# Non-local attention on one core: query tiles in pairs on halves of TensorE, and a constant in place of the row maximum

## The chip, the cores and the metric

The kernel runs on one core of one Trainium2 chip. The core has TensorE (PE, matrix multiply, which writes to the accumulator memory PSUM), VectorE (DVE, elementwise work and reductions), ScalarE (ACT, functions such as exp), GpSimd (POOL) and the queues that start DMA transfers. The metric is the device time of one execution in microseconds (us), lower being better. The median of three runs of the kernel before is 6832.08 us (6814.51 to 6840.58).

## The reference: what is computed

Two layers of a "non-local block" on `x` of shape (4, 128, 96, 96): four images of 128 channels and 96 x 96 = 9216 pixels, all in f32. One layer, with its own weights:

```
g_x     = maxpool2(g_w @ x + g_b)          # 64 channels x 2304 pooled pixels: the values
theta_x = theta_w @ x + theta_b            # 64 channels x 9216 pixels: the queries
phi_x   = maxpool2(phi_w @ x + phi_b)      # 64 channels x 2304 pooled pixels: the keys
f       = theta_x^T phi_x                  # 9216 x 2304 scores
attn    = softmax(f) over the 2304 keys
y       = attn g_x^T                       # 9216 x 64
out     = (W_w @ y + W_b) * inv + (bn_beta - bn_mean * inv) + x     # inv = bn_gamma / sqrt(bn_var + 1e-5)
```

The second layer takes the first one's output. The scores and the product with the values are nearly all the work: 2 x 64 x 9216 x 2304 multiplications for each layer and image. A softmax is unchanged when one number is subtracted from all scores of a row, or when one vector is subtracted from all keys.

## The kernel before, in words

An image stays on chip through both layers; the four images follow each other, and the next one's load is started a whole image early. `block` does one layer of one image, so there are eight blocks.

A block begins with `keys_and_values`: 24 matmuls (`gphi_ps`, L128) give g and phi for 384 pixels each, ACT adds the bias (`full`, L132), DVE takes the 2 x 2 maximum in two steps (`half`, `gphi`). `spread` (L143) copies phi to the other half of the partitions (`phi1`) and transposes g into `gT`, 18 tiles of 128 keys, each with 64 columns of g and 64 columns of ones.

Then come 18 query tiles of 512 pixels. A tile goes through two stages:

- `stage1`: theta (L172); the scores with queries on partitions, 24 matmuls of 64 rows x 384 columns (`max_ps`, L179), in pairs of which one takes partitions 0 to 63 (`phi`) and the other 64 to 127 (`gphi`); DVE reduces each to a row maximum (`mx`, L188); four transposes turn the negated maximum into a 65th row of theta (`m_ps`, L198; L199).
- `stage2`: for each of 18 key tiles the scores again, now with keys on partitions (`sc`, L246, 65 rows, so that the maximum is subtracted), exp on ACT (L250), and the product with `gT` into the accumulator `av` (L260). Its columns of ones give the softmax denominators on partitions 64 to 127.

`finish` takes four reciprocals (L217), multiplies (`y`, L220), projects with W (`W_ps`, L224) and adds shift and residual (L225). The order is written out by hand: in `stage2` the step for key tile k issues the scores of tile k+1, then the steps of `finish` for the tile before and of `stage1` for the tile after that are due at k (the dictionaries `steps`), then the product for tile k. A scheduler keeps this order on each engine except at the borders between blocks, where it moves work that is ready ahead. Every f32 matmul appears in the trace as two records of TensorE, each with its own weight load.

Of the kernel before, what the change touches and what calls it, by code (L numbers as in the profile page):

```python
# [8 lines left out]

F32 = mybir.dt.float32  # L10
AF = mybir.ActivationFunctionType
ALU = mybir.AluOpType
AX = mybir.AxisListType
PSUM = bass.MemoryType.PSUM

P = 128
B, C, CI, H, W = 4, 128, 64, 96, 96
HW = H * W
NK = (H // 2) * (W // 2)
QT = 512  # L20
NQ = HW // QT
KT = 128
NKT = NK // KT
GT = 6
CC = 4 * W
MC = 384
NMC = NK // MC
BN_EPS = 1e-5
PARAMS = ["g_w", "g_b", "theta_w", "theta_b", "phi_w", "phi_b", "W_w", "W_b",
          "bn_gamma", "bn_beta", "bn_mean", "bn_var"]  # L30


@with_exitstack
def nonlocal_blocks(ctx: ExitStack, tc: tile.TileContext, x: bass.AP, layers, out: bass.AP):
    """Two non-local blocks over 4 images; an image stays on chip through both.

    A query tile of 512 pixels goes through two stages:
      1. theta, the scores with queries on partitions, and their row maximum m;
      2. the scores with keys on partitions, -m added by a 65th contraction row, exp,
         and the product with g^T, whose 64 columns of ones give the denominators  # L40
         on 64 partitions.
    Stage 1 of a tile is interleaved with stage 2 of the tile before it.
    """
    nc = tc.nc

    const = ctx.enter_context(tc.tile_pool(name="const", bufs=1))
    prep = ctx.enter_context(tc.tile_pool(name="prep", bufs=2))
    xp = ctx.enter_context(tc.tile_pool(name="xp", bufs=2))
    yp = ctx.enter_context(tc.tile_pool(name="yp", bufs=1))
    kvp = ctx.enter_context(tc.tile_pool(name="kvp", bufs=2))  # L50
    work = ctx.enter_context(tc.tile_pool(name="work", bufs=3))
    ps_max = ctx.enter_context(tc.tile_pool(name="ps_max", bufs=3, space=PSUM))
    ps_sc = ctx.enter_context(tc.tile_pool(name="ps_sc", bufs=2, space=PSUM))
    ps_av = ctx.enter_context(tc.tile_pool(name="ps_av", bufs=2, space=PSUM))
    ps_misc = ctx.enter_context(tc.tile_pool(name="ps_misc", bufs=1, space=PSUM))

    ident = const.tile([P, P], F32, name="ident")
    make_identity(nc, ident)
    eps = const.tile([P, 1], F32, name="eps")
    nc.vector.memset(eps, BN_EPS)  # L60

    def load_x(b):
        xt = xp.tile([C, HW], F32, tag="x", name=f"x_{b}")
        src = x[b].rearrange("c h w -> c (h w)")
# [51 lines left out]
        return w  # L116

    def keys_and_values(xt, w, name):
        """g^T beside columns of ones, and phi on both halves of the partitions."""
        gphi = kvp.tile([P, NK], F32, tag="gphi", name=f"gphi_{name}")  # L120
        phi1 = kvp.tile([CI + 1, NK], F32, tag="phi1", name=f"phi1_{name}")
        gT = kvp.tile([P, NKT, 2 * CI], F32, tag="gT", name=f"gT_{name}")
        nc.gpsimd.memset(phi1[CI:, :], 1.0)
        nc.gpsimd.memset(gT[:, :, CI:], 1.0)

        def pooled(r):
            ps = ps_sc.tile([P, QT], F32, tag="sc", name=f"gphi_ps_{name}_{r}")
            nc.tensor.matmul(  # L128
                ps[:, :CC], lhsT=w["gphi"], rhs=xt[:, ts(r, CC)], start=True, stop=True
            )  # L130
            full = work.tile([P, CC], F32, tag="full", name=f"full_{name}_{r}")
            nc.scalar.activation(full, ps[:, :CC], AF.Identity, bias=w["gphi_b"])  # L132
            half = work.tile([P, CC // 2], F32, tag="half", name=f"half_{name}_{r}")
            fv = full.rearrange("p (n d) -> p n d", d=2)
            nc.vector.tensor_max(half, fv[:, :, 0], fv[:, :, 1])
            hv = half.rearrange("p (h d w) -> p h d w", d=2, w=W // 2)
            nc.vector.tensor_max(
                gphi[:, ts(r, CC // 4)].rearrange("p (h w) -> p h w", w=W // 2),
                hv[:, :, 0],
                hv[:, :, 1],  # L140
            )

        def spread(i):  # L143
            keys = ts(i, GT * KT)
            nc.scalar.copy(phi1[:CI, keys], gphi[CI:, keys])
            ps = ps_max.tile([P, QT], F32, tag="mx", name=f"gT_ps_{name}_{i}")
            for j in range(GT):
                nc.tensor.transpose(  # L148
                    ps[:, ts(j, CI)], gphi[:CI, ts(i * GT + j, KT)], ident[:CI, :CI]
                )  # L150
            nc.vector.tensor_copy(
                gT[:, ts(i, GT), :CI],
                ps[:, : GT * CI].rearrange("p (t c) -> p t c", c=CI),
            )

        per = GT * KT * 4 // CC
        for r in range(HW // CC):
            pooled(r)
            if r % per == 0 and r:
                spread(r // per - 1)  # L160
        spread(NKT // GT - 1)
        return gphi, phi1, gT

    def stage1(xt, w, phis, name):
        """The query tile [theta; -m], and the steps that fill it."""
        th = work.tile([P, QT], F32, tag="theta", name=f"theta_{name}")
        mx = work.tile([P, QT // P, NMC], F32, tag="mxs", name=f"mx_{name}")
        nm = work.tile([P, QT // P], F32, tag="nm", name=f"nm_{name}")

        def theta():  # L170
            ps = ps_misc.tile([P, QT], F32, tag="misc", name=f"theta_ps_{name}")
            nc.tensor.matmul(ps, lhsT=w["theta"], rhs=xt, start=True, stop=True)  # L172
            nc.scalar.activation(th, ps, AF.Identity, bias=w["theta_b"])  # L173

        def pair(a, c):
            pss = []
            for h in range(2):
                ps = ps_max.tile([P, QT], F32, tag="mx", name=f"max_ps_{name}_{a}_{c + h}")
                nc.tensor.matmul(  # L179
                    ps[:, :MC],  # L180
                    lhsT=th[ts(h, CI), ts(a, P)],
                    rhs=phis[h][ts(h, CI), ts(c + h, MC)],
                    start=True,
                    stop=True,
                )
                pss.append(ps)
            for h in range(2):
                nc.vector.tensor_reduce(  # L188
                    mx[:, a, c + h : c + h + 1], pss[h][:, :MC], AX.X, ALU.max
                )  # L190

        def negmax():
            nc.vector.tensor_reduce(nm, mx, AX.X, ALU.max, negate=True)  # L193

        def row():
            ps = ps_misc.tile([P, QT], F32, tag="misc", name=f"m_ps_{name}")
            for a in range(QT // P):
                nc.tensor.transpose(ps[:1, ts(a, P)], nm[:, a : a + 1], ident)  # L198
            nc.scalar.copy(th[CI : CI + 1, :], ps[:1, :])  # L199

        steps = {0: theta}
        n = 2
        for a in range(QT // P):
            for c in range(0, NMC, 2):
                steps[n] = lambda a=a, c=c: pair(a, c)
                n += 1
        steps[n] = negmax
        steps[n + 2] = row
        return th, steps

    def finish(av, xt, w, dst, store, name):
        """The steps from the summed products to the block's output."""
        rc = work.tile([CI, QT], F32, tag="rc", name=f"rc_{name}")
        y = work.tile([CI, QT], F32, tag="y", name=f"y_{name}")

        def recip(i):
            nc.vector.reciprocal(rc[:, ts(i, P)], av[CI:, ts(i, P)])  # L217

        def norm():
            nc.vector.tensor_mul(y, av[:CI, :], rc)  # L220

        def project():
            ps = ps_misc.tile([P, QT], F32, tag="misc", name=f"W_ps_{name}")
            nc.tensor.matmul(ps, lhsT=w["W"], rhs=y, start=True, stop=True)  # L224
            nc.vector.scalar_tensor_tensor(  # L225
                dst, ps, w["shift"], xt, op0=ALU.add, op1=ALU.add
            )
            if store is not None:
                nc.sync.dma_start(out=store, in_=dst)

        steps = {i: (lambda i=i: recip(i)) for i in range(QT // P)}
        steps[QT // P] = norm
        steps[QT // P + 2] = project
        return steps
# [53 lines left out]
    xt = load_x(0)  # L288
    ws = [load_layer(l, p) for l, p in enumerate(layers)]
    for b in range(B):  # L290
        nxt = load_x(b + 1) if b + 1 < B else None
# [3 lines left out]
        xt = nxt  # L295


# [1 line left out]
_INS = ["x"] + [f"L{l}_conv_{p}" for l in range(2) for p in PARAMS]  # L299
_OUTS = [((B, C, H, W), "float32")]  # L300
# [25 lines left out]
```

## Time and profile before

| what | value |
|---|---|
| time, median of 3 runs | 6832.08 us (6814.51, 6832.08, 6840.58) |
| profiled execution, span from first to last instruction | 6810.1 us |
| TensorE busy | 6758.3 us, 99% |
| VectorE busy | 2595.4 us, 38% |
| ScalarE busy | 1862.6 us, 27% |
| DMA | 41.21 MB, mean 6 GB/s |
| mean granted clock of TensorE | 0.999 of full speed |

The profiled execution's page gives its span and no other time; by the three runs what lies around the span is between 4.4 and 30.5 us, and 22.0 us to the median. Records of matmuls overlap each other at their ends, so the length of a step on TensorE is read from the starts of successive records or from the chain of waits (which follows the work back from the last instruction and gives each piece only the time until the next begins), not from the mean duration.

### The profile page before, as it was taken

How to read it: one execution, taken by the hardware profiler on the slowest of the kernel's cores; microseconds unless marked ns; L12 is line 12 of the kernel's file. 1: busy time of each engine (PE TensorE's matmuls, PEld its weight loads, DVE VectorE, ACT ScalarE, POOL GpSimd, SP SyncE). 2: the span in 40 equal slices, each digit the busy share in tenths (PEclk: the TensorE clock that was granted, in tenths of full speed). 3: DMA queues.
4: the chain of work that ended last, by engine and by line, in shares of the span. 5: the costliest groups of instructions: out<-in, count | busy, mean ns of one | idle time of the engine just before them, and what ended most of it. 6: DMA issues, size and time to landing. Idle time of an engine off the chain costs nothing.

```text
span 6810.1 us, 48920 instructions
## 1 busy us (share of the span) xinstructions
PE 6758.3 (99%) x18966; PEld 2603.7 (38%) x18966; DVE 2595.4 (38%) x4889; ACT 1862.6 (27%) x3100; POOL 25.2 (0%) x22
## 2 busy tenths in 40 slices
PE   8999999999999999999999999999999999999999
PEld 3333333333333333333333333333333333333333
DVE  3333343333433334333343333433334333343333
ACT  2222232222322223222232222322223222222222
POOL 0000000000000000000000000000000000000000
PEclk9999999999999999999999999999999999999999
DMA  1000000000000000000000000000000000000000
GB/s 58 0 0 0 0 30 7 7 7 5 3 1 0 0 0 31 5 7 7 7 2 0 0 0 0 4 7 5 7 7 2 0 0 0 0 4 7 7 5 8
DMA packets 17065, 41.21 MB, mean 6 GB/s; under 512 B 4032, under 2 KB 4544, under 8 KB 16832
## 3 DMA queue, kind: packets, MB, share of 16 engines
q1 hardware_dynamic: 13824, 37.75, 1.5%
q8 instruction: 148, 2.42, 0.1%
q10 hardware_dynamic: 3008, 0.34, 0.0%
q14 instruction: 85, 0.70, 0.0%
HBM read 19.21 MB, written 18.87 MB: 6 GB/s over the span
## 4 chain that ended last, share of the span: by engine, by line
PE 99%; DVE 1%; DMA 0%; ACT 0%; issue 0%; ACTq 0%
PE av L260 37%; PE sc L246 33%; PE max_ps L179 22%; PE theta_ps L172 2%; PE gphi_ps L128 2%; PE W_ps L224 2%; PE m_ps L198 1%; DVE rc L217 0%; PE gT_ps L148 0%; DMA W_nat<-in_L_conv_W_w_dram 0%; DVE mx L188 0%; ACT full L132 0%; DMA theta_b<-in_L_conv_theta_b_dram 0%; DMA gphi_nat<-in_L_conv_phi_w_dram 0%; ACT theta L199 0%
## 5 line engine op out<-in xcount | busy, mean ns | idle before, releaser
L188 DVE TENSOR_REDUCE mx<-max_ps 128x1 f32<-128x384 f32 x3456 | 1763.8, 552 | 2804.5 <-PE max_ps L179 2800.0
L250 ACT ACTIVATE exp<-sc 128x512 f32<-128x512 f32 x2592 | 1547.7, 597 | 4696.7 <-PE sc L246 4696.7
L260 PE MATMUL av<-exp,gT 128*128 128x512 f32 x5184 | 2796.9, 625 | 0.0
L246 PE MATMUL sc<-theta,phi 65*128 65x512 f32 x5184 | 2628.6, 592 | 5.9 <-ACT theta L199 5.9
L179 PE MATMUL max_ps<-gphi,theta 64*128 64x384 f32 x3456 | 1570.6, 535 | 0.0
L179 PE MATMUL max_ps<-phi,theta 64*128 64x384 f32 x3456 | 1556.3, 531 | 4.0 <-DVE mx L188 3.1
L246 PEld LDWEIGHTS sc<-theta,phi 65*128 65x128 f32 x5184 | 986.3, 190 | 1247.0 <-issue 1213.4
L260 PEld LDWEIGHTS av<-exp,gT 128*128 128x128 f32 x5184 | 835.0, 188 | 1295.3 <-ACT exp L250 866.8
L179 PEld LDWEIGHTS max_ps<-phi,theta 64*128 64x128 f32 x3456 | 518.9, 185 | 1230.1 <-DVE mx L188 958.0
L217 DVE RECIPROCAL rc<-av 64x128 f32<-64x128 f32 x576 | 488.7, 908 | 1003.0 <-PE av L260 1003.0
L179 PEld LDWEIGHTS max_ps<-gphi,theta 64*128 64x128 f32 x3456 | 508.6, 184 | 18.1 <-DVE mx L188 16.7
L224 PE MATMUL W_ps<-y,WT 64*128 64x512 f32 x288 | 162.6, 644 | 4.2 <-DVE y L220 4.2
L132 ACT ACTIVATE full<-gphi_ps,gphi_b 128x384 f32<-128x384 f32 x192 | 110.7, 581 | 73.2 <-PE gphi_ps L128 50.3
L225 DVE SCALAR_TENSOR_TENSOR out<-W_ps,shift,y 128x512 f32<-128x512 f32 x72 | 54.0, 751 | 164.3 <-PE W_ps L224 164.3
L225 DVE SCALAR_TENSOR_TENSOR y<-W_ps,shift,x 128x512 f32<-128x512 f32 x72 | 54.1, 751 | 162.5 <-PE W_ps L224 162.5
L199 ACT COPY theta<-m_ps 1x512 f32<-1x512 f32 x144 | 82.5, 573 | 106.3 <-PE m_ps L198 103.0
L173 ACT ACTIVATE theta<-theta_ps,theta_b 128x512 f32<-128x512 f32 x144 | 99.0, 688 | 30.5 <-PE theta_ps L172 30.5
L220 DVE TENSOR_TENSOR y<-av,rc 64x512 f32<-64x512 f32 x144 | 98.2, 682 | 4.9
L198 PE MATMUL m_ps<-ident,nm 128*1 128x128 f32 x576 | 86.4, 271 | 6.9 <-DVE nm L193 6.9
L128 PE MATMUL gphi_ps<-x,gphiT 128*128 128x384 f32 x192 | 82.7, 542 | 7.6 <-ACT full L132 4.7
L224 PEld LDWEIGHTS W_ps<-y,WT 64*128 64x128 f32 x288 | 42.6, 185 | 111.9 <-issue 103.1
L198 PEld LDWEIGHTS m_ps<-ident,nm 128*1 128x1 f32 x576 | 47.0, 83 | 99.5 <-issue 80.0
(40 smaller groups left out, 598.0 us busy)
## 6 DMA issues: line engine op xcount, KB each, us to landing
x<-in_x_dram SPq DMA_DIRECT2D x24, 768.0 KB, 7.2
out_dram<-out SPq DMA_DIRECT2D x72, 256.0 KB, 2.0
theta_nat<-in_L_conv_theta_w_dram ACTq DMA_DIRECT2D x4, 32.0 KB, 5.3
theta_b<-in_L_conv_theta_b_dram ACTq DMA_DIRECT2D x4, 0.2 KB, 5.8
gphi_nat<-in_L_conv_g_w_dram ACTq DMA_DIRECT2D x2, 32.0 KB, 5.3
gphi_nat<-in_L_conv_phi_w_dram ACTq DMA_DIRECT2D x2, 32.0 KB, 4.2
W_nat<-in_L_conv_W_w_dram ACTq DMA_DIRECT2D x2, 32.0 KB, 7.4
gphi_b<-in_L_conv_g_b_dram ACTq DMA_DIRECT2D x2, 0.2 KB, 5.1
```

Of the source, the lines that this page charges most:

```text
L128: nc.tensor.matmul(ps[:, :CC], lhsT=w["gphi"], rhs=xt[:, ts(r, CC)], start=True, stop=True)
L132: nc.scalar.activation(full, ps[:, :CC], AF.Identity, bias=w["gphi_b"])
L172: nc.tensor.matmul(ps, lhsT=w["theta"], rhs=xt, start=True, stop=True)
L179: nc.tensor.matmul(ps[:, :MC], lhsT=th[ts(h, CI), ts(a, P)], rhs=phis[h][ts(h, CI), ts(c + h, MC)], start=True, stop=True,)
L188: nc.vector.tensor_reduce(mx[:, a, c + h : c + h + 1], pss[h][:, :MC], AX.X, ALU.max)
L198: nc.tensor.transpose(ps[:1, ts(a, P)], nm[:, a : a + 1], ident)
L217: nc.vector.reciprocal(rc[:, ts(i, P)], av[CI:, ts(i, P)])
L224: nc.tensor.matmul(ps, lhsT=w["W"], rhs=y, start=True, stop=True)
L225: nc.vector.scalar_tensor_tensor(dst, ps, w["shift"], xt, op0=ALU.add, op1=ALU.add)
L246: nc.tensor.matmul(ps, lhsT=phi1[:, ts(k, KT)], rhs=th[: CI + 1, :], start=True, stop=True)
L250: nc.scalar.activation(e, ps, AF.Exp)
L260: nc.tensor.matmul(av, lhsT=gT[:, k, :], rhs=es.pop(k), start=(k == 0), stop=(k == NKT - 1))
```

## The change

The kernel has a new main path, `shifted_blocks`. The old path is kept as `general_blocks`, word for word but for comments, and stands behind a branch.

- Two query tiles form a pair of 1024 queries. Theta of the first is written to partitions 0 to 63, of the second to 64 to 127 (`theta`). The scores of one key tile (`Pair.scores`) are two matmuls of 64 rows: phi on partitions 0 to 63 with the first tile, phi on 64 to 127 with the second; they fill a PSUM tile of 128 x 1024, and one exp covers both. The products (`Pair.values`) are two matmuls with 64 columns of `gT`: the first tile's go to partitions 0 to 63 of `av`, the second's to 64 to 127.
- The row maximum is not computed. Exp subtracts the constant 35, and phi is centred: the mean of its first 768 keys is subtracted from all. `stage1`'s 24 matmuls and reductions, the maximum's transposes and the 65th row are gone.
- The columns of ones are gone too: DVE sums the exp tiles (`sum`), one add of 128 x 1024 for each key tile but the first, and two matmuls with a matrix of ones (`denominators`) add them over the partitions. Reciprocals and `y` now cover 128 partitions, that is, a pair.
- DVE keeps the largest and smallest reciprocal (`rmax`, `rmin`). At the end they are compared with 1e20 and 1e-30, a flag is written, every engine loads it, and if it is above zero `general_blocks` runs and writes the output anew.
- Pooling is one DVE reduction out of PSUM; g's bias is added after pooling, phi's is left out. The first layer's output is written over `x` in place.
- The order by hand: batches of two key tiles. A step issues the scores of a batch, a W projection if due, then the products of the batch before, then theta or denominators if due.

```diff
+PT = 2 * QT
+NP = HW // PT
+KB = 2
+NB = NKT // KB
+SHIFT = 35.0
+SUM_MIN, SUM_MAX = 1e-20, 1e30
...
+    ps_sc = ctx.enter_context(tc.tile_pool(name="ps_sc", bufs=2, space=PSUM))
+    ps_av = ctx.enter_context(tc.tile_pool(name="ps_av", bufs=2, space=PSUM))
+    ps_misc = ctx.enter_context(tc.tile_pool(name="ps_misc", bufs=2, space=PSUM))
...
+        def pooled(r):
+            ps = ps_sc.tile([P, PT], F32, tag="sc", name=f"gphi_ps_{name}_{r}")
+            nc.tensor.matmul(
+                ps[:, :CC], lhsT=w["gphi"], rhs=xt[:, ts(r, CC)], start=True, stop=True
+            )
+            nc.vector.tensor_reduce(
...
+            if i == 0:
+                nc.vector.tensor_reduce(centre[CI:, :], gphi[CI:, keys], AX.X, ALU.add)
...
+            nc.scalar.activation(
+                phi[CI:, keys], gphi[CI:, keys], AF.Identity, bias=centre[CI:, :]
+            )
+            nc.scalar.copy(phi[:CI, keys], phi[CI:, keys])
...
+    def theta(xt, w, p, name):
+        ps = ps_misc.tile([P, QT], F32, tag="misc", name=f"theta_ps_{name}_{p}")
+        for h in range(2):
+            nc.tensor.matmul(
+                ps[ts(h, CI), :], lhsT=w["theta"], rhs=xt[:, ts(2 * p + h, QT)],
+                start=True, stop=True,
+            )
+        th = work.tile([P, QT], F32, tag="theta", name=f"theta_{name}_{p}")
+        nc.scalar.activation(th, ps, AF.Identity, bias=w["theta_b"])
...
+        def scores(self, k):
+            ps = ps_sc.tile([P, PT], F32, tag="sc", name=f"sc_{self.name}_{k}")
+            for h in range(2):
+                nc.tensor.matmul(
+                    ps[:, ts(h, QT)], lhsT=self.phi[ts(h, CI), ts(k, KT)],
+                    rhs=self.th[ts(h, CI), :], start=True, stop=True,
+                )
+            e = work.tile([P, PT], F32, tag="exp", name=f"exp_{self.name}_{k}", bufs=6)
+            nc.scalar.activation(e, ps, AF.Exp, bias=nshift)
+            self.es[k] = e
+            if k == 1:
+                self.sum = work.tile([P, PT], F32, tag="sum", name=f"sum_{self.name}")
+                nc.vector.tensor_add(self.sum, self.es[0], e)
+            elif k > 1:
+                nc.vector.tensor_add(self.sum, self.sum, e)
+
+        def values(self, k):
...
+            for h in range(2):
+                nc.tensor.matmul(
+                    self.av[ts(h, CI), :], lhsT=self.gT[:, k, :], rhs=e[:, ts(h, QT)],
+                    start=(k == 0), stop=(k == NKT - 1),
+                )
+
+        def denominators(self):
...
+            for i in range(QT // P):
+                nc.vector.reciprocal(rc[:, ts(i, P)], ps[:, ts(i, P)])
+            self.y = work.tile([P, QT], F32, tag="y", name=f"y_{self.name}")
+            nc.vector.tensor_mul(self.y, self.av, rc)
+            nc.vector.tensor_tensor(rmax, rmax, rc, ALU.max)
+            nc.vector.tensor_tensor(rmin, rmin, rc, ALU.min)
...
+        for t in range(len(batches) + 1):
+            if t < len(batches):
+                p, j = batches[t]
+                for k in range(j * KB, (j + 1) * KB):
+                    pairs[p].scores(k)
+            for step in hooks.pop((t, "rows"), []):
+                step()
+            if t:
+                p, j = batches[t - 1]
+                for k in range(j * KB, (j + 1) * KB):
+                    pairs[p].values(k)
+                if j == NB // 2 and p + 1 < NP:
+                    pairs[p + 1] = pair(p + 1)
+                if j == NB - 1:
+                    done = pairs.pop(p)
+                    hooks.setdefault((t + 1, "columns"), []).append(done.denominators)
+                    hooks.setdefault((t + 4, "rows"), []).append(done.project)
+            for step in hooks.pop((t, "columns"), []):
+                step()
...
+def nonlocal_blocks(tc: tile.TileContext, x: bass.AP, layers, out: bass.AP):
+    with tc.tile_pool(name="flag", bufs=1) as pool:
+        flag = pool.tile([1, 1], I32, name="flag")
+        shifted_blocks(tc, x, layers, out, flag)
+        bad = tc.nc.values_load(flag[0:1, 0:1])
+        with tc.If(bad > 0):
+            general_blocks(tc, x, layers, out)
```

How the instructions stand on an engine is shown at three places. A row is a line of the program, the operation, what it writes and what it reads, and the shape of the output; "x2" is two such in a row.

First place, TensorE in the middle of a query tile. Before, two key tiles of tile 10 with the maximum's matmuls of tile 11 between them:

```order
L179 MATMUL max_ps_0_11_0_0_2364<-phi_0_0_200,theta_0_11_2336 128x384
L179 MATMUL max_ps_0_11_0_1_2366<-gphi_0_199,theta_0_11_2336 128x384
L260 MATMUL av_0_10_2339<-exp_0_10_2_2355,gT_0_201 128x512
L246 MATMUL sc_0_10_4_2371<-theta_0_10_2150,phi_0_0_200 128x512
L179 MATMUL max_ps_0_11_0_2_2376<-phi_0_0_200,theta_0_11_2336 128x384
L179 MATMUL max_ps_0_11_0_3_2378<-gphi_0_199,theta_0_11_2336 128x384
L260 MATMUL av_0_10_2339<-exp_0_10_3_2361,gT_0_201 128x512
L246 MATMUL sc_0_10_5_2383<-theta_0_10_2150,phi_0_0_200 128x512
```

Now, two batches of pair 5, with the denominators of pair 4 between them:

```order
L221 MATMUL sc_1_5_2_12565<-theta_1_5_12499,phi_1_11611 128x512 x2
L221 MATMUL sc_1_5_3_12571<-theta_1_5_12499,phi_1_11611 128x512 x2
L239 MATMUL av_1_5_12577<-exp_1_5_0_12552,gT_1_11612 64x512 x2
L239 MATMUL av_1_5_12577<-exp_1_5_1_12557,gT_1_11612 64x512 x2
L247 MATMUL den_1_4_12582<-sum_1_4_12389,ones 64x512 x2
L221 MATMUL sc_1_5_4_12594<-theta_1_5_12499,phi_1_11611 128x512 x2
L221 MATMUL sc_1_5_5_12600<-theta_1_5_12499,phi_1_11611 128x512 x2
```

The matmuls of the maximum are gone from between the products and scores. Four matmuls on halves of the rows now alternate with four on halves of the columns, and the denominators and theta join a run on columns, W a run on rows.

Second place, VectorE where a tile or pair ends. Before:

```order
L188 TENSOR_REDUCE mx_0_14_2895<-max_ps_0_14_3_4_3048 128x1
L188 TENSOR_REDUCE mx_0_14_2895<-max_ps_0_14_3_5_3050 128x1
L193 TENSOR_REDUCE nm_0_14_2896<-mx_0_14_2895 128x4
L217 RECIPROCAL rc_0_13_3078<-av_0_13_2897 64x128 x4
L220 TENSOR_TENSOR y_0_13_3079<-av_0_13_2897,rc_0_13_3078 64x512
L188 TENSOR_REDUCE mx_0_15_3081<-max_ps_0_15_0_0_3108 128x1
```

Now, where pair 1 ends and pair 2 runs:

```order
L232 TENSOR_TENSOR sum_0_2_10427<-sum_0_2_10427,exp_0_2_3_10442 128x1024
L253 RECIPROCAL rc_0_1_10453<-den_0_1_10450 128x128 x4
L232 TENSOR_TENSOR sum_0_2_10427<-sum_0_2_10427,exp_0_2_4_10465 128x1024
L255 TENSOR_TENSOR y_0_1_10458<-av_0_1_10277,rc_0_1_10453 128x512
L256 TENSOR_TENSOR rmax<-rmax,rc_0_1_10453 128x512
L257 TENSOR_TENSOR rmin<-rmin,rc_0_1_10453 128x512
L232 TENSOR_TENSOR sum_0_2_10427<-sum_0_2_10427,exp_0_2_5_10471 128x1024
```

The adds of the running pair stand where the reductions stood, and the reciprocals of the pair before come in between two of them.

Third place, TensorE at the border of two blocks. Before, after the last product of a block:

```order
L260 MATMUL av_0_17_3638<-exp_0_17_17_3733,gT_0_201 128x512
L128 MATMUL gphi_ps_1_0_3752<-y_0_198,gphiT_163 128x384
L128 MATMUL gphi_ps_1_1_3759<-y_0_198,gphiT_163 128x384
L128 MATMUL gphi_ps_1_2_3766<-y_0_198,gphiT_163 128x384
L128 MATMUL gphi_ps_1_3_3773<-y_0_198,gphiT_163 128x384
L128 MATMUL gphi_ps_1_4_3780<-y_0_198,gphiT_163 128x384
L128 MATMUL gphi_ps_1_5_3787<-y_0_198,gphiT_163 128x384
L224 MATMUL W_ps_0_17_3744<-y_0_17_3738,WT_143 128x512
```

Now:

```order
L239 MATMUL av_0_8_1665<-exp_0_8_17_1793,gT_0_204 64x512 x2
L247 MATMUL den_0_8_1804<-sum_0_8_1647,ones 64x512 x2
L156 MATMUL gphi_ps_1_0_1826<-x_98,gphiT_164 128x384
L156 MATMUL gphi_ps_1_1_1829<-x_98,gphiT_164 128x384
L156 MATMUL gphi_ps_1_2_1832<-x_98,gphiT_164 128x384
L267 MATMUL W_ps_0_8_0_1816<-y_0_8_1812,WT_147 128x512
L267 MATMUL W_ps_0_8_1_1818<-y_0_8_1812,WT_147 128x512
L156 MATMUL gphi_ps_1_3_1835<-x_98,gphiT_164 128x384
```

Three pooling matmuls instead of six stand between the last product and the projection that ends the block; the denominators' matmuls are new there.

## Rows read from the trace of the kernel before

**Rows 1.** The page: span, and busy time of each engine.

```profile
span 6810.1 us, 48920 instructions
PE 6758.3 (99%) x18966; PEld 2603.7 (38%) x18966; DVE 2595.4 (38%) x4889; ACT 1862.6 (27%) x3100; POOL 25.2 (0%) x22
```

**Rows 2.** The page: chain that ended last, share of the span by line.

```profile
PE av L260 37%; PE sc L246 33%; PE max_ps L179 22%; PE theta_ps L172 2%; PE gphi_ps L128 2%; PE W_ps L224 2%; PE m_ps L198 1%; DVE rc L217 0%; PE gT_ps L148 0%; DMA W_nat<-in_L_conv_W_w_dram 0%; DVE mx L188 0%; ACT full L132 0%; DMA theta_b<-in_L_conv_theta_b_dram 0%; DMA gphi_nat<-in_L_conv_phi_w_dram 0%; ACT theta L199 0%
```

**Rows 3.** Chain of waits, in order of time: start, length (us), piece; inside a tile.

```profile
3002.52 0.84 PE max_ps L179 x4
3003.37 1.06 PE av L260 x2
3004.42 0.86 PE sc L246 x2
```

**Rows 4.** Timeline of TensorE: start, duration (us); one pair of the maximum's matmuls.

```profile
3007.97 0.59 PE L179 MATMUL max_ps<-phi,theta 64*128 64x384 f32 x1
3007.98 0.59 PE L179 MATMUL max_ps<-gphi,theta 64*128 64x384 f32 x1
3008.40 0.48 PE L179 MATMUL max_ps<-phi,theta 64*128 64x384 f32 x1
3008.41 0.48 PE L179 MATMUL max_ps<-gphi,theta 64*128 64x384 f32 x1
```

**Rows 5.** Timeline of TensorE where a projection and such a pair meet.

```profile
2506.11 0.69 PE L224 MATMUL W_ps<-y,WT 64*128 64x512 f32 x1
2506.12 0.91 PE L179 MATMUL max_ps<-gphi,theta 64*128 64x384 f32 x2
2507.07 0.81 PE L179 MATMUL max_ps<-phi,theta 64*128 64x384 f32 x2
```

**Rows 6.** Chain of waits where the maximum is transposed (one column of weights).

```profile
3013.39 0.86 PE sc L246 x2
3014.25 0.44 PE m_ps L198 x4
3014.68 1.72 PE av L260 x4
```

**Rows 7.** Groups: line, engine, op, names, shapes, count; busy us, mean ns; idle before.

```profile
L250 ACT ACTIVATE exp<-sc 128x512 f32<-128x512 f32 x2592 | 1547.7, 597 | 4696.7 <-PE sc L246 4696.7
L173 ACT ACTIVATE theta<-theta_ps,theta_b 128x512 f32<-128x512 f32 x144 | 99.0, 688 | 30.5 <-PE theta_ps L172 30.5
L135 DVE TENSOR_TENSOR half<-full 128x192 f32<-128x192 f32 x192 | 66.7, 353 | 30.9 <-ACT full L132 29.5
L220 DVE TENSOR_TENSOR y<-av,rc 64x512 f32<-64x512 f32 x144 | 98.2, 682 | 4.9
L225 DVE SCALAR_TENSOR_TENSOR out<-W_ps,shift,y 128x512 f32<-128x512 f32 x72 | 54.0, 751 | 164.3 <-PE W_ps L224 164.3
L217 DVE RECIPROCAL rc<-av 64x128 f32<-64x128 f32 x576 | 488.7, 908 | 1003.0 <-PE av L260 1003.0
L188 DVE TENSOR_REDUCE mx<-max_ps 128x1 f32<-128x384 f32 x3456 | 1763.8, 552 | 2804.5 <-PE max_ps L179 2800.0
```

**Rows 8.** Chain of waits at the border of the first two blocks.

```profile
872.23 1.89 PE av L260 x4
874.14 3.39 DVE rc L217 x4
878.48 0.91 PE gphi_ps L128 x2
897.35 0.59 ACT full L132
```

**Rows 9.** Chain of waits in the first block: maximum's first matmuls, first scores.

```profile
52.45 0.96 PE max_ps L179 x3
66.92 1.98 PE sc L246 x4
```

**Rows 10.** Chain of waits at the end: last projection.

```profile
6804.05 2.08 PE W_ps L224 x2
```

More of the change, by code (lines that the diff above doesn't have):

```diff
@@ L10 @@
 F32 = mybir.dt.float32
+I32 = mybir.dt.int32
 AF = mybir.ActivationFunctionType
@@ L44, in nonlocal_blocks, with general_blocks @@
+@with_exitstack
+def general_blocks(ctx: ExitStack, tc: tile.TileContext, x: bass.AP, layers, out: bass.AP):
     nc = tc.nc
```

177 lines of the change are left out of this document (176 added, 1 removed).

## The prediction, on record before the changed kernel ran

> **What bounds the kernel now.** I read the page first: TensorE is busy 99% of a span of 6810.1 us, VectorE 38%, ScalarE 27% [rows 1]. Busy time alone proves little, since matmul records overlap, so the chain of waits comes next: 37% of the span stands on the product with the values, 33% on the scores, 22% on the row maximum, all on TensorE [rows 2]. Nothing waits for long on another engine. What a matmul costs is thus read from the chain and from starts of records, and the change is worth what it takes off TensorE, as long as the other engines stay under the new length of a step.
>
> Three prices come from there. A matmul of 512 columns on the full array takes 0.86 us, 0.43 for each of its two records (L246, L260; [rows 3, 6]). A step with a pair of the maximum's matmuls takes 0.84 + 1.06 + 0.86 = 2.76 us [rows 3]. The pair itself shows that halves of the rows work side by side: `phi` starts at 3007.97, `gphi` at 3007.98, their second records at 3008.40 and 3008.41 [rows 4]. At 0.43 per 512 columns, 384 columns in two records would be 0.645 us, for both halves together. The step without the pair is 1.72, so 2.76 - 1.72 - 0.645 = 0.395 us is paid for going from the full array to halves of rows and back: about 0.2 for each switch. I take this 0.2 as the price of a switch between halves of rows and any other shape. That it is not paid at every change of shape is seen where the maximum is transposed with one column of weights: 0.86, 0.44, 1.72, no step longer than its records [rows 6].
>
> **The change part by part, for one pair (1024 queries); there are 72.**
> Removed: 48 maximum matmuls with their switches, 48 reductions, eight transposes, and the 65th row.
>
> Scores: 18 key tiles of two matmuls on halves of the rows. Side by side, as in [rows 4], a key tile takes 0.86: 15.5 us. The program before needed 36 x 0.86.
>
> Products: 18 key tiles of two matmuls on halves of the columns. No row of before shows two matmuls on halves of the columns at once. Bounds: 0.86 per key tile if they run like the row halves, 1.72 one behind the other. I take 0.86, the value of the nearest rows, which are the row halves: 15.5 us.
>
> The Trainium skill (TensorE: Matmul & The Clock Gate, table under "Measured speedup vs the span model") has three column tiles at 2.38 times the speed of one by one, that is 79% of the ideal; an estimate from this page is 0.86 / 0.79 = 1.09 per key tile and 290 us more in all. The sum here keeps 0.86.
>
> Theta, denominators and W: two matmuls each, side by side, 0.86 each: 2.6 us.
>
> Switches: a batch of two key tiles goes from rows to columns and back, nine batches, 9 x 0.395 = 3.6 us. Theta, denominators and W stand inside a run of their own shape and add no switch. Bounds: 0 as at [rows 6], and 0.4 per switch (twice the row). I take 0.2, because halves of rows are one side of each switch here as there.
>
> TensorE per pair: 15.5 + 15.5 + 2.6 + 3.6 = 37.1 us; 72 pairs: 2671 us.
>
> Is it hidden? ScalarE: an exp of 512 columns takes 597 ns; theta's activation, which has a bias operand as the new exp has, 688 [rows 7]. An exp of 1024 costs at most 2 x 0.69 = 1.38. With theta that is 18 x 1.38 + 0.7 = 25.5 us of the 37.1. The latency counts too, because there are two PSUM tiles of scores: the second matmul of the next batch overwrites what the second exp reads. A batch takes 2 x 1.72 + 0.395 = 3.84 us. The first score tile is complete some 1.3 us after the batch begins (switch, 0.86, tail of the record, a semaphore), both exps are done at 1.3 + 2.76 = 4.1, and their second buffer is wanted at 3.84 + 0.2 + 0.86 = 4.9. It fits, up to 1.8 us for an exp.
>
> VectorE: 192 columns take 353 ns and 512 take 682 [rows 7], so 1024 take 682 + 512 x 329 / 320 = 1.21 us. 17 adds are 20.6, four reciprocals 3.6 (0.908; that 128 partitions cost what 64 did is my assumption), `y`, `rmax`, `rmin` 2.0 (0.68 each), the two residual adds 1.5 (0.751): 27.7 us of 37.1. The upper bound for an add, from the slowest operation of 512 columns, is 2 x 0.751 = 1.5: 32.7 us, still under. Where a pair ends, 5.7 us of reciprocals, `y`, `rmax` and `rmin` come into the adds. Six exp buffers are three batches, so an add may be some 8 us late before an exp waits for its buffer. That costs nothing. If this cover is gone (adds above 1.76 us), VectorE sets the pair.
>
> The max pass of the first block goes: first maximum matmul at 52.45, first scores at 66.92 [rows 9], and without it the scores can begin at about 54.
>
> Seven borders between blocks: before, 874.14 to 897.35 plus what follows until phi is spread [rows 8], 23.2 us, under which five pooling matmuls run beside the reciprocals. Now VectorE does the pooling and stands in the reciprocals itself, two score buffers hold two pooled tiles, so three pooling matmuls get ahead instead of five (+1.3); `rmax`, `rmin` and the reductions (0.552 each) delay the rest by 2; centring, a first exp and a filling pipeline cost 1.5 more. W and theta in this stretch (1.9) are counted with the pairs. 23.2 + 4.8 - 1.9 = 26; 7 x 26 = 182 us. Bounds: 15.5 (24 pooling matmuls of 384 columns alone) to 35 (twice the added delay and more).
>
> The end: reciprocals 3.4, `y`, `rmax`, `rmin` 2.0, the last W 2.1 [rows 10], residual 1.5, some seven small instructions for the flag, its load on each engine, the branch. I take 15; the load and the branch are in no row, from 1 to 30 us.
>
> DMA is the same; its 6 GB/s hide anywhere.
>
> Sum: 54 + 2671 + 182 + 15 = 2922 us of span, against the span of 6810.1. The median of the runs lies 22.0 above this span, so I forecast 2944, rounded to 2940.
>
> **The rivals.**
> 1. Column halves do not overlap. For it: no row shows them doing so; products, theta and denominators read different data on all 128 rows at once. Against it: the row halves do run together. Price: 18 + 2 times 0.86 more per pair, 17.2 us, 1238 in all: 4180 us.
> 2. Halves overlap, but start in program order, so that the second half of a batch begins one record late. For the products alone 9 x 0.43 x 72 = 279: 3220 us; for scores too, 557: 3500. The trace speaks against it for rows: the program issues W, then `phi`, then `gphi`, and `gphi` starts at 2506.12, beside W and 0.95 us ahead of `phi`, which needs W's rows [rows 5]. So each half of the rows goes at its own pace; of columns no row tells. The Trainium skill (TensorE: Matmul & The Clock Gate, "The mechanism") says that matmuls start and end strictly in program order; by that rule it would be 3500 us, and [rows 5] disagrees with it.
> 3. Switches between halves of rows and of columns cost nothing, as with one column of weights [rows 6]: 72 x 3.6 = 256 less, 2680 us. The Trainium skill (TensorEngine Tiling (Array Packing), "Key Properties") has every change of tiling mode drain the engine. [rows 3] agree, [rows 6] do not.
> 4. ScalarE or VectorE becomes the bound: two exps and their waits, or late adds, stretch a batch from 3.84 to some 4.35 us. 9 x 0.5 x 72 = 324: 3260 us. Against it the margins above.
> 5. Slower than before: the flag comes out above zero, and the old path runs after the new one. Place: the branch at the end; price: the old span, 2940 + 6810 = 9750 us. It decides as soon as one sum of 9216 x 8 lies outside 1e-20 to 1e30. Worked out from the reference's inputs, the shifted sums lie between 2e-10 and 1.1e15, ten and fifteen decades inside.
>
> **How the numbers follow.** Forecast 0.64, with a range of its own of 2800 to 3100 (a switch from 0.1 to 0.3 us is 130 either way, borders and end 60). Rival 1: 0.10. Rival 2: 0.09, mostly products alone. Rival 3: 0.09. Rival 4: 0.06. Rival 5: 0.02. The range of 2660 to 3280 us takes in the forecast, rival 3, rival 4 and most of rival 2, some 0.85; left out are 4180, 3500 and 9750. About 0.5% is what a measurement of this kernel can tell from no change. Every case but the last is faster by far more, so faster 0.97; within 0.5% 0.01, for something not thought of; slower 0.02.
>
> **What would show it.** In the profile of the changed kernel: two product records (L239) starting within some 10 ns of each other and again 0.43 later (rival 1: 0.86 for each half by itself; rival 2: the second half 0.43 behind); a batch of two key tiles every 3.84 us; between the last score and first product some 0.2 us more than a record; no wait of scores for exp that lasts; exp at 1.0 to 1.4 us, adds at 1.2; VectorE busy 70 to 75%, ScalarE 50 to 65%; a border of 26 us beyond the pairs; and only some microseconds after the last residual add. The prediction is wrong if a pair takes more than 40 us or less than 34, whatever the sum.

## The result, and the profile after

The changed kernel takes 2915.31 us (median of four runs, 2911.15 to 2916.18). Against the kernel before that is a ratio of 0.4269 (95% interval 0.426 to 0.4279). The forecast was 2940 us, 0.8% above, with a range of 2660 to 3280.

The page of the changed kernel, as [rows 1, 2] for the kernel before: span, busy time of each engine, and the chain that ended last by line.

```profile
span 2913.7 us, 29776 instructions
...
PE 2842.7 (98%) x11768; PEld 913.5 (31%) x11768; DVE 2071.7 (71%) x2131; ACT 1467.4 (50%) x1420; POOL 1.6 (0%) x8
...
PE sc L221 42%; PE av L239 41%; PE gphi_ps L156 4%; PE theta_ps L200 2%; PE W_ps L267 2%; PE den L247 2%; DVE rc L253 1%; DVE gphi L159 1%; PE gT_ps L179 1%; DMA theta_b<-in_L_conv_theta_b_dram 0%; ACT exp L226 0%; DVE centre L169 0%; ACT phi L173 0%; DMA W_nat<-in_L_conv_W_w_dram 0%; ACT phi L176 0%; DMA theta_nat<-in_L_conv_theta_w_dram 0%
```

TensorE still sets the end, and VectorE's busy share has gone from 38 to 71%. The maximum, 22% of the old chain, is gone, and scores and products together take 83% of a span that is less than half as long.

The chain of waits inside a pair (start, length in us, piece) answers to [rows 3]:

```profile
1503.52 1.92 PE sc L221 x8
1505.44 1.87 PE av L239 x8
1507.31 1.92 PE sc L221 x8
1509.22 1.87 PE av L239 x8
1511.09 0.86 PE theta_ps L200 x4
...
1547.73 0.86 PE theta_ps L200 x4
```

Eight records are four matmuls, two key tiles for both query tiles. Four on row halves take 1.92 = 2 x 0.86 + 0.20, four on column halves 1.87 = 2 x 0.86 + 0.15. So two matmuls run at once in both, and what is left over stands at the switch. Theta joins the products' run and costs 0.86, nothing more. From one `theta_ps` (1511.09) to the next (1547.73) a pair takes 36.64 us.

That column halves start together, and not one behind the other, is seen in the timeline of TensorE at the begin of such a run:

```profile
1501.59 0.65 PE L239 MATMUL av<-exp,gT 128*64 128x512 f32 x2
```

Two records of 0.59 to 0.64 us cover 0.65 us between them: they start within 0.06 us of each other.

The groups that answer to [rows 7] (busy us, mean ns; idle before, and what ended it):

```profile
L226 ACT ACTIVATE exp<-sc,nshift 128x1024 f32<-128x1024 f32 x1296 | 1372.5, 1110 | 1083.7 <-PE sc L221 1083.5
L232 DVE TENSOR_TENSOR sum<-sum,exp 128x1024 f32<-128x1024 f32 x1152 | 1406.3, 1221 | 556.6 <-ACT exp L226 492.2
...
L253 DVE RECIPROCAL rc<-den 128x128 f32<-128x128 f32 x288 | 243.7, 908 | 12.8 <-PE den L247 12.8
```

Neither ScalarE nor VectorE sets the pace: ScalarE waits for TensorE's scores, 1083 us in all, and VectorE for ScalarE's exps, 492 us before the adds.

### The profile page after: what moved, and what is told of

Its sections match the earlier page's. It is cut to its first block, busy times and chain, and to the rows that moved or that the text cites. A ratio compares the mean times of both kernels' runs of the same rounds, so it can differ in the third digit from the quotient of the medians.

```text
span 2913.7 us, 29776 instructions
## 1 busy us (share of the span) xinstructions
PE 2842.7 (98%) x11768; PEld 913.5 (31%) x11768; DVE 2071.7 (71%) x2131; ACT 1467.4 (50%) x1420; POOL 1.6 (0%) x8
## 4 chain that ended last, share of the span: by engine, by line
PE 95%; DVE 2%; ACT 1%; DMA 1%; issue 0%; ACTq 0%
PE sc L221 42%; PE av L239 41%; PE gphi_ps L156 4%; PE theta_ps L200 2%; PE W_ps L267 2%; PE den L247 2%; DVE rc L253 1%; DVE gphi L159 1%; PE gT_ps L179 1%; DMA theta_b<-in_L_conv_theta_b_dram 0%; ACT exp L226 0%; DVE centre L169 0%; ACT phi L173 0%; DMA W_nat<-in_L_conv_W_w_dram 0%; ACT phi L176 0%; DMA theta_nat<-in_L_conv_theta_w_dram 0%
## 5 line engine op out<-in xcount | busy, mean ns | idle before, releaser
L226 ACT ACTIVATE exp<-sc,nshift 128x1024 f32<-128x1024 f32 x1296 | 1372.5, 1110 | 1083.7 <-PE sc L221 1083.5
L232 DVE TENSOR_TENSOR sum<-sum,exp 128x1024 f32<-128x1024 f32 x1152 | 1406.3, 1221 | 556.6 <-ACT exp L226 492.2
L221 PE MATMUL sc<-theta,phi 64*128 64x512 f32 x5184 | 1289.0, 615 | 12.6 <-ACT exp L226 8.0
L239 PE MATMUL av<-exp,gT 128*64 128x512 f32 x5184 | 1253.5, 605 | 0.0
L221 PEld LDWEIGHTS sc<-theta,phi 64*128 64x128 f32 x5184 | 445.3, 186 | 840.3 <-issue 457.3
L239 PEld LDWEIGHTS av<-exp,gT 128*64 128x64 f32 x5184 | 315.0, 136 | 859.8 <-issue 853.7
L253 DVE RECIPROCAL rc<-den 128x128 f32<-128x128 f32 x288 | 243.7, 908 | 12.8 <-PE den L247 12.8
L230 DVE TENSOR_TENSOR sum<-exp,exp 128x1024 f32<-128x1024 f32 x72 | 88.2, 1225 | 175.7 <-ACT exp L226 175.7
L156 PE MATMUL gphi_ps<-x,gphiT 128*128 128x384 f32 x384 | 170.5, 556 | 35.6 <-DVE gphi L159 30.5
L159 DVE TENSOR_REDUCE gphi<-gphi_ps 128x96 f32<-128x384 f32 x192 | 105.5, 554 | 62.7 <-PE gphi_ps L156 57.5
```

What stands on the lines that cost most here:

```text
L156: nc.tensor.matmul(ps[:, :CC], lhsT=w["gphi"], rhs=xt[:, ts(r, CC)], start=True, stop=True)
L159: nc.vector.tensor_reduce(gphi[:, ts(r, CC // 4)].rearrange("p (h w) -> p h w", w=W // 2), ps[:, :CC].rearrange("p (h a w b) -> p h w a b" ...
L221: nc.tensor.matmul(ps[:, ts(h, QT)], lhsT=self.phi[ts(h, CI), ts(k, KT)], rhs=self.th[ts(h, CI), :], start=True, stop=True,)
L226: nc.scalar.activation(e, ps, AF.Exp, bias=nshift)
L230: nc.vector.tensor_add(self.sum, self.es[0], e)
L232: nc.vector.tensor_add(self.sum, self.sum, e)
```

## The experiments

**The maximum alone: before_no_max.** The kernel before, without its row maximum.

```diff
-        steps = {0: theta}
...
-        steps[n] = negmax
-        steps[n + 2] = row
-        return th, steps
+        def constant():
+            nc.gpsimd.memset(th[CI : CI + 1, :], -15.0)
+
+        return th, {0: theta, 2: constant}
```

> The kernel before without its row maximum: the 24 matmuls of 64 rows and 24 reductions of each tile, the transposes and the maximum's row are left out, the 65th row is a constant written by GpSimd (the scores are shifted by it, and W is multiplied by zero to keep the second layer's numbers small). Theory: the maximum costs what it takes on TensorE, 12 x (2.76 - 1.72) + 0.44 = 12.9 us of the 45.6 us of a tile, and some 14 us at each block's start: 144 x 32.7 + 130 = 4840 us. Rival: part of the maximum ran beside other work and its removal brings less: above 5500 us. So the halves of rows and columns together would have brought the rest, from 4840 to 2915.

Measured: 5001.89 us, ratio 0.733 (0.7305 to 0.7356). The direction holds, the size was 160 us off. From one projection to the next a tile takes 33.22 us:

```profile
1503.28 1.05 PE W_ps L219 x2
1504.33 1.06 PE av L255 x2
...
1536.50 1.05 PE W_ps L219 x2
```

33.22 instead of 32.7 is 144 x 0.52 = 75 us of the miss. Most of the 0.52 is W. Before, it stood beside a pair of the maximum [rows 5] and shared that pair's switches: both together took 1.70 us (2506.18 to 2507.88 in the chain), W adding its bare 0.86. Now it pays for switches of its own, 1.05 for W and 1.06 for the product behind it instead of 0.86 each. The rest is my account of what lies around the tiles: the last tile of a block carried no maximum, so the 45.6 us held for 136 of 144 tiles only, and some 8 x 12.5 = 100 us more lie outside. At the medians the maximum was worth 1810 us (6812.23 - 5001.89; the kernel before ran again beside this run) of the 3897 us that the change gained (6812.23 - 2915.31). Everything else in the change, the halves of rows and columns above all, brought the other 2087.

**Products on the full array: cols_full.**

```diff
-                    self.av[ts(h, CI), :], lhsT=self.gT[:, k, :], rhs=e[:, ts(h, QT)],
-                    start=(k == 0), stop=(k == NKT - 1),
+                    self.av, lhsT=self.gT[:, k, :], rhs=e[:, ts(h, QT)],
+                    start=(k == 0 and h == 0), stop=(k == NKT - 1 and h == 1),
```

> The changed kernel with products on the full array: g stands twice in the weights (128 columns), both matmuls of a pair go one behind the other into all of av (the output is the sum of both tiles' products; W is multiplied by zero). Theory: column halves run side by side and are worth one slot of 0.86 us for each key tile, 15.5 us a pair, and a switch back costs 0.2 instead of 0.15: 36.64 + 15.5 + 0.45 = 52.6 us a pair, 72 pairs and the same 275 us around them: 4060 us. Rival: products are not what sets the step (exp or the adds do): near 2915 us, at most 3300.

Measured: 4076.25 us, ratio 0.5974 (0.5953 to 0.5995). Its chain of waits:

```profile
1507.27 1.92 PE sc L222 x8
1509.19 3.63 PE av L240 x8
```

Four products take 3.63 = 4 x 0.86 + 0.19 instead of 1.87. This is what rival 1 would have looked like. The column halves are worth 1161 us, and the theory's 4060 is 0.4% off. Theta and denominators stayed on halves here; rival 1 counted them too.

**Scores on all rows: rows_full.**

```diff
-                    ps[:, ts(h, QT)], lhsT=self.phi[ts(h, CI), ts(k, KT)],
-                    rhs=self.th[ts(h, CI), :], start=True, stop=True,
+                    ps[:, ts(h, QT)], lhsT=self.phi[:, ts(k, KT)],
+                    rhs=self.th, start=True, stop=True,
```

> The changed kernel with scores on all 128 rows: phi of both halves against theta of both tiles, one matmul behind the other (the scores are the sum of two tiles'; shift 70; flag not loaded, no branch). Theory: row halves are worth 15.5 us a pair, and the price of switches goes with the halves of rows, so full rows against halves of columns switch for nothing, as the one-column transposes did before; only W, still on row halves, switches: 36.64 + 15.5 - 9 x 0.345 + 0.4 = 49.4 us a pair, 3835 us. Rival: any change of shape costs 0.15 to 0.2 us: 52.1 us a pair, 4030 us.

Measured: 4030.15 us (4019.11 and 4041.19), ratio 0.5906 (0.5878 to 0.5934). Here my theory fell and the rival's 4030 came true; the two runs lie 22 us apart, so that it came true to the microsecond is luck. Chain of waits:

```profile
1727.84 3.63 PE sc L221 x8
1731.47 1.06 PE W_ps L267 x4
1732.53 1.87 PE av L239 x8
1734.40 3.63 PE sc L221 x8
```

There are no row halves but W's, and still the scores' run takes 0.19 more than 4 x 0.86, the products' 0.15 more than 2 x 0.86, and W 0.20 more than 0.86. The price is paid at any change between these shapes, not for row halves alone. The Trainium skill (TensorEngine Tiling (Array Packing), "Key Properties") has every change of tiling mode drain the engine; these rows agree, with 0.34 us for a round trip between 128 and 64 columns.

**Batches of one key tile: kb1.**

```diff
-KB = 2
+KB = 1
...
-                    hooks.setdefault((t + 1, "columns"), []).append(done.denominators)
-                    hooks.setdefault((t + 4, "rows"), []).append(done.project)
+                    hooks.setdefault((t + 2, "columns"), []).append(done.denominators)
+                    hooks.setdefault((t + 8, "rows"), []).append(done.project)
```

> The changed kernel with batches of one key tile instead of two, denominators and projection moved so that they come as late in time as before. Theory: 18 round trips between rows and columns instead of 9, each 0.345 us: 3.1 us a pair more, 224 in all: 3140 us. Rival: the 0.345 us is a wait for exp that happens once a batch and is hidden or shorter when batches are short: 2915 us or less. Second rival: short batches leave too little time for exp, and TensorE waits for it: above 3300 us.

Measured: 3147.2 us (3143.75 to 3148.34), ratio 0.4611 (0.4599 to 0.4624). Chain of waits:

```profile
1499.68 1.06 PE sc L221 x4
1500.74 1.01 PE av L239 x4
```

1.06 = 0.86 + 0.20 and 1.01 = 0.86 + 0.15: the same price, twice as often. It stands at the switch and is no wait for exp.

**VectorE's cover: half_adds and adds_twice.** In the first, after the add of the first two key tiles only odd ones are added; in the second, each add but the first stands twice.

```diff
-            elif k > 1:
+            elif k % 2:
                 nc.vector.tensor_add(self.sum, self.sum, e)
```

> The changed kernel with half of VectorE's adds left out: only exp tiles of odd key tiles are summed (the denominators are wrong; W is multiplied by zero). VectorE loses 8 x 1.22 = 9.8 us a pair. Theory: its work is hidden in the pairs, TensorE sets them: the same time, 2905 to 2915 us. Rival: the adds hold exp buffers up where a pair ends, and TensorE loses time there: 2850 us or less.

Measured: 2912.05 us (2908.18 to 2915.9), ratio 0.4266 (0.4257 to 0.4276). The page of half_adds:

```profile
PE 2840.8 (97%) x11768; PEld 912.9 (31%) x11768; DVE 1393.0 (48%) x1555; ACT 1468.3 (50%) x1420; POOL 1.6 (0%) x8
```

VectorE does 679 us less, and the time stays within the runs' spread. Its adds were hidden.

> The changed kernel with each add but the first done twice (the sums are wrong by a factor that divides out only in part). VectorE then has 27.9 + 16 x 1.22 = 47.4 us a pair against TensorE's 36.6. Theory: VectorE sets the pair, 72 x 47.4 = 3413 us and some 240 around: 3650 us. Rival: VectorE's work counts only in part, since instructions overlap at their ends (0.1 us each): 3550 us; or exp buffers run dry and both engines wait in turn: above 3800 us.

Measured: 3742.05 us (3736.86 and 3747.24), ratio 0.5485 (0.5468 to 0.5501). The chain of waits now runs over VectorE, from one pair's reciprocals on:

```profile
1536.51 1.24 DVE sum L232
1537.77 1.24 DVE sum L233
1539.10 1.23 DVE sum L232
1543.05 1.71 DVE rc L254 x2
...
1591.55 1.71 DVE rc L254 x2
```

48.5 us a pair (1543.05 to 1591.55) instead of the 47.4 expected; from start to start the adds take 1.26 and 1.33 in turn, not 1.22. 72 x 1.1 is 79 of the 92 us missing. So the cover is real. Where it ends was not found: the changed kernel's 27.9 us of VectorE a pair are hidden, and the doubled adds' 48.5 are not. TensorE's mean granted clock was 0.926 in this run, but the chain of this pair has no piece of TensorE.

**Filling the border: stream and stream_cols.** The step loop runs over all blocks, and the next block's pooling, one matmul a step, stands behind products of the last three pairs.

```diff
+        for r in range(HW // CC):
+            t = start + r if r < 21 or not same else t0 + per + 4
+            at(t, "columns", lambda m=m, r=r: keys[m].pooled(r))
...
+    batches = [(n, p, j) for n in range(len(blocks)) for p in range(NP) for j in range(NB)]
```

> The changed kernel with the border between blocks filled: the pooling of the next block (one matmul and one reduction at a time) is put behind the products of the last three pairs of the block before, into the PSUM tiles of theta and W; scores of the next block follow at once, only the last three pooling matmuls of the same image wait for the last projection. The arithmetic is the same. Theory: a block takes 9 x 36.64 = 329.8 us and 31.0 or 28.5 us more at a border; of these some 18 to 20 are matmuls and transposes that stay, 10 to 12 are waits for the reciprocals, half-clock matmuls and the phi copies, which go: 7 x 11 = 77 us less, 2840 us. Rival: the inserted matmuls wait for PSUM tiles behind the adds on VectorE, and what is won at the border is lost in the pairs: 2915 us or more.

Measured: 2880.27 us (2879.46 to 2882.66), ratio 0.4223 (0.4215 to 0.4231): faster than the changed kernel by 35 us, less than half of the expected 75. The chain of waits of stream shows the larger part of the reason:

```profile
343.86 1.87 PE av L244 x8
345.73 0.84 PE gphi_ps L156 x2
346.57 1.92 PE sc L226 x8
```

A pooling matmul of 384 columns would take 0.645; it takes 0.84; 24 x 7 x 0.19 = 32 us, of 40 missing. I had put it between products and scores as if the step from 64 columns to the full array were free. rows_full had shown in the meantime that it isn't.

> The filled border again (stream, 2880 us), with two edits. Each pooling matmul is split into two on halves of the columns (g's weights, phi's weights, the same pixels), so that it joins the run of the products; and the phi copies are issued later, where VectorE has no backlog. Theory: in stream each pooling matmul between products and scores took 0.84 us, 0.645 and one more switch of 0.2; 24 x 7 x 0.2 = 33 us of that go, and some 10 us of waits of exp behind phi copies: 2837 us. Rival: both halves read the same pixels and go one behind the other, 0.645 us more each: 2970 us. Second rival: the 40 us by which stream missed its 2840 are waits at the borders and not switches: 2870 us or more.

```diff
+            for h in range(2):
+                nc.tensor.matmul(
+                    ps[ts(h, CI), :CC], lhsT=self.w["gphi"][:, ts(h, CI)],
+                    rhs=self.xt[:, ts(r, CC)], start=True, stop=True,
+                )
```

Measured: 2847.39 us (2846.2 to 2851.22), ratio 0.4174 (0.4164 to 0.4183). Chain of waits:

```profile
348.19 1.87 PE av L246 x8
350.06 0.65 PE gphi_ps L157 x4
350.70 1.92 PE sc L228 x8
```

The same work on column halves takes 0.65, without a switch, and both halves read the same pixels at once. This version beats the kernel before and the changed one (by 68 us, 2.3%). The run moved two things, the column halves and the later phi copies; by the estimate above the switch is some 32 of the 33 us between the two versions, which leaves next to nothing for the copies. No run has one without the other.

## Why the prediction was right, step by step

*Removed, scores, products.* Right, and for the reason given: 0.86 us for a key tile of a pair in either kind of half. For columns no row of before had shown it; the nearest row, the row halves, was the right guide, and cols_full shows that without it, for the products alone, the time would be 4076 (rival 1, with theta and denominators: 4180). Rival 2 falls with the timeline's row at 1501.59 and with runs of two slots instead of two and a half.

*Switches.* 0.395 a batch was predicted, 0.35 measured: 0.20 into the scores, 0.15 into the products. The pair came out at 36.64 instead of 37.1, 33 us less over 72. So the term stood nearly right. What failed is the reading set beside it from [rows 6], that the price goes with halves of rows and a change without them is free. Rival 3 took the same rows for the switches between halves. rows_full and stream, expected from this reading, missed by 195 and 40 us.

[rows 6] do show a free change: four transposes of 128 columns would take 0.43 us at 0.43 per 512 columns (an estimate from [rows 3]), and their run lasts 0.44. But they do not speak for weights of 64 or 128 columns. The timeline shows a difference in the weight loads (PEld). Before, at the transposes:

```profile
3013.66 0.08 PEld L198 LDWEIGHTS m_ps<-ident,nm 128*1 128x1 f32 x1 [0.24 <-issue]
3014.08 0.60 PE L198 MATMUL m_ps<-ident,nm 128*1 128x128 f32 x4
```

In the changed kernel, at a switch into the products:

```profile
1505.37 0.20 PEld L239 LDWEIGHTS av<-exp,gT 128*64 128x64 f32 x4 [0.76 <-issue]
1505.37 1.94 PE L239 MATMUL av<-exp,gT 128*64 128x512 f32 x8
```

The first load stands 0.42 us ahead of its matmul there, under other work, and starts together with it here. A load takes 186 ns on average for the scores and 136 for the products, close to the 0.20 and 0.15 of a switch. That the price is this uncovered load, and not something else that comes with the change of shape, fits these rows; no run tried it.

*Cover.* Right: an add 1.221 us (1.21 predicted), a reciprocal on 128 partitions 908 ns as on 64, an exp 1.110 (at most 1.38). half_adds shows VectorE hidden, adds_twice shows that the cover does end.

*Start.* First scores at 47.5 us (54 predicted).

*Borders.* Mis-sized: 26 us predicted, 30.3 measured. From the denominators at the first border (377.12) to those at the seventh (2537.36) a block takes 2160.24 / 6 = 360.04 us, less nine pairs of 36.64. One thing that was too small is the centring, put at 1.5 together with the first exp and the filling. At the first border, in the chain of waits:

```profile
392.14 0.57 DVE gphi L159
...
392.74 0.95 DVE centre L169
...
395.56 1.56 PE gphi_ps L156 x4
```

The sum over 768 keys stands among the pooling reductions on VectorE, and with the first values' copy the chain runs over VectorE for 3.4 us. TensorE was not idle all that time: between 392.24 and 395.56 it did work that takes 0.84 + 0.26 + 1.49 = 2.59 us at other places of this chain, so it lost some 0.7 us. Another is the head start under the reciprocals: only two pooling matmuls ran there, not three. The third had to wait 2.42 us for a reduction behind the reciprocals (381.89).

What was missing altogether is TensorE's clock. Busy times of the engines in four stretches of that border, with the granted clock behind them:

```profile
382.00:384.00 2.00, 2.00 (x6) 0.48 (x6) 1.62 (x3) 0.00 (x0) 0.00 (x0) 0.78 0.00 0
384.00:386.00 2.00, 0.61 (x3) 0.17 (x2) 1.50 (x3) 0.00 (x0) 0.00 (x0) 0.50 0.00 0
386.00:388.00 2.00, 2.00 (x4) 0.81 (x5) 1.32 (x3) 0.00 (x0) 0.00 (x0) 0.50 0.00 0
388.00:390.00 2.00, 2.00 (x4) 0.88 (x3) 0.63 (x2) 0.00 (x0) 0.00 (x0) 0.52 0.04 8
```

The columns are stretch, length, busy us of PE, PEld, DVE, ACT and POOL with the number of instructions, granted clock, DMA share and GB/s. After TensorE had stood idle under the reciprocals (379.5 to 381.9), the granted clock was at 0.50, the lower of its two levels (1.2 GHz), for some six microseconds, and W took 1.72 us there. The same pieces of the chain at the first border and at the second, where the granted clock stayed at 1.00:

```profile
382.80 1.72 PE W_ps L267 x4
...
385.86 1.62 PE gphi_ps L156 x2
387.48 0.30 PE gT_ps L179
387.77 2.58 PE gphi_ps L156 x4
```

```profile
744.08 1.11 PE W_ps L267 x4
...
746.54 0.88 PE gphi_ps L156 x2
747.42 0.20 PE gT_ps L179
747.62 1.52 PE gphi_ps L156 x4
```

They differ by 0.61 + 0.74 + 0.10 + 1.06 = 2.5 us. From the denominators to the second scores' run the first border lasts 35.95 us, the third and fifth 35.96, the seventh 35.90; the second, fourth and sixth, with the same work but another image's pixels behind them, take 33.46. The clock fell to 0.50 in the third, fifth and seventh too, and stayed at 1.00 in the fourth and sixth. The 2.5 us of difference are thus the clock's. A border at full clock is still 358.79 - 329.76 = 29.0 us (738.41 to 1097.20, less nine pairs), 3 more than predicted; some 0.7 of them are the centring and 0.6 the third pooling matmul, and the rest was not itemised.

*End.* 14.2 us from the end of the denominators to the last instruction (15 predicted). The last instruction in the chain is the flag's cast:

```profile
2898.59 0.88 PE den L247 x4
...
2906.11 1.41 DVE out L273 x2
...
2907.61 0.14 DVE flag L329
```

The load of the flag and the branch fit into the 6 us between it and 2913.7, and the old path did not run: rival 5 is out.

*The sum.* 47.5 + 72 x 36.64 + 7 x 30.3 + 14.2 = 2912 us, against 2922 predicted and a span of 2913.7. The errors of pairs, borders and start (-33, +30, -6.5) cancel in part, so that the sum is closer than its terms is luck. One term had no ground at all: the 22.0 us between span and median. The profiled run took 2915.95 us for its span of 2913.7, so 2.25 lie around it. In later runs the kernel before took 6812.23 us with a span of 6810.4, and in others its span was itself longer (6836.4, 6828.0); what I had added was the difference between two executions. Around the span of the kernel before lie 1.8 us, not 4.4 to 30.5. Of the 25 us between forecast and result some 20 are this term.

## What to carry to other kernels

Where a matmul uses half of TensorE's rows or columns, give the other half to an equal piece of other data; then count the changes of shape, put works of one shape in one run, and cut small work to the shape of its neighbours, as the pooling here (0.84 to 0.65 us). A switch that is free between two shapes says nothing of another pair of shapes: look in the timeline where the weight loads stand at both. A piece of the chain on another engine does not mean that TensorE stood idle for its length; look at its records. And take the time around a span from a run whose span you have, not from the median of others.

## What the runs showed of the hardware that was not expected

- The changes between weights of 64 rows x 128 columns, of 128 x 64 and of the full array that these rows show cost 0.20 us into scores, W or the full array and 0.15 into products, in the changed kernel, cols_full, rows_full, kb1 and stream. The price lies near the mean length of the new weights' load (186 to 202 ns, and 136), which starts with the run instead of ahead of it. The transposes of g in the changed kernel bear this out: their weights have 128 columns, but load in 139 ns, and the switch into them costs 0.14 (0.20 us for one record, 0.26 for two, so 0.06 a record). Between works of one shape (products, denominators, theta) a change cost nothing.
- The two halves of the columns read the same data in SBUF at once (stream_cols) or different data (products) at the same speed: 0.65 us for 384 columns, 0.86 for 512.
- The granted clock fell to 0.50 at the first border and not at the second, though TensorE had waited 2.42 us at the same place in both (up to 381.9 and up to 743.2). In this execution it fell at the four borders between the two layers of one image and at none of the three between images. Why only there stays open.
